# A graph layer on one core: all instruction orders replaced, and a restart charge in the planner

## The chip, the core and the metric

The kernel runs on one core of a Trainium2 chip. A core has five engines that run side by side, each with its own queue of instructions: TensorE (PE in the profile; its loading of the stationary matrix is listed apart as PEld), VectorE (DVE), ScalarE (ACT), GpSimd (POOL) and SyncE (SP), which here issues all the DMAs. An engine takes its instructions strictly in the order in which the program lists them, and waits on semaphores for what other engines produce. The metric is the device time in microseconds of one execution; less is better.

## The reference

For each of 64 graphs with 256 tokens of 768 features, the layer normalizes the tokens, multiplies them by three weight matrices, and sums over the edges of the graph in both directions:

```python
h = jnp.maximum(_layernorm(x, axis=-1), 0.0)
adj = heads.astype(hs.dtype); radj = jnp.swapaxes(adj, 1, 2)
ctx = jnp.matmul(adj, hs @ Wadj.T + badj) / deg_c[..., None]
ctx = ctx + jnp.matmul(radj, hs @ Wrev.T + brev) / rdeg_c[..., None]
ctx = ctx + hs @ Wself.T + bself
agg = jnp.einsum('bij,bijr->bir', adj, E[rels])
rel = agg @ Wr.T + br * deg[..., None]
...
return ctx + rel        # and x + that is the output
```

Adjacency and relation are the same 0/1 array, so that the relation terms come down to degrees of the tokens times a few fixed rows. (The kernel counts whether any other value occurs, and would then take a general path, which doesn't run here.)

## The kernel before, in words

**The mathematics.** A graph's tokens form two chunks of 128, `a` and `b`; the features form three blocks of 256 (`a0`, `a1`, `a2` and `b0`, `b1`, `b2`). The weights form three by three blocks. Instead of 18 block products for one image (that is, one graph) the kernel makes 15 (`PRODUCTS`, L24): GpSimd adds blocks of activations (L585), VectorE and ScalarE prepared sums of weight blocks once. For precision each operand is split into words (`split`, L590: ScalarE makes `left0`, VectorE `left1` and `left2`), and a product is three passes of four matmuls of 128x384: `first` and `second`, of 4 and 8 matmuls or the reverse, with a rescaling of the PSUM bank by ScalarE between them (`scale`, L657).

**The PSUM banks.** There are four double banks (class Q in `SLOTS`, L80). Several products share one, one after the other, and make a chain: x, y, z, w, t, u, v. After each product a `read` adds the bank into a result `c`: VectorE at L677 or L679, ScalarE at L668 for the first. The bank is free when the chain's last read is done.

**The two sweeps.** The weights of 15 products don't fit beside the rest, so there are two sweeps over the images. The first (`step1`) makes products 10, 5, 2, 8, 11, 14, 3 and 13 and stores five partial results and h in DRAM. Then the prepared weights are exchanged. The second (`step2`) loads them back, makes products 9, 7, 6, 15, 12, 4 and 1, adds the fixed rows (`rows`, L647), and multiplies by the adjacency: `aggregate` (L909) makes four groups of 8 matmuls (L917), `agg10`, `agg11`, `agg00` and `agg01`, from high and low words of `c` (ScalarE L901, GpSimd L905), each into a bank of its own that VectorE reads with L928. The first and the last image run in another way (`whole`, L754); the other 62 are regular.

**The front of an image** (`front1`): statistics (L698, L702), a power on GpSimd (L706), a transposition on PE (L709), a copy to DRAM and a broadcast back (`row`, L719), then GpSimd centres h (L728) and VectorE normalizes it (L732). In the second sweep there is a transposition of the degrees (L886).

**The order of the instructions** isn't written out. `record` (L416) lists every operation with its engine, an assumed duration, the buffers it reads and writes, and a due time, its `rank`: a time within the image plus the image's start. To each rank `Plan.op` (L270) adds an entry of the table `OFFSETS` (L91), by the kind of operation: `first 4` or `agg11` for all regular images alike, with suffixes `@`, `@1`, `$1` and `$` for the first two and last two images. Then `Plan.schedule` (L303) runs through modelled time: whenever an engine is idle, it takes from those operations whose inputs are known to be ready and whose buffers are free the one with the least rank; the engine is then idle again at the operation's modelled end less a fixed overlap (`OVERLAP`, L85; 0.17 us for PE). The order in which operations are picked is the order in which they are emitted, and so fixes the queue of every engine, SP's among them, and which buffer takes which slot.

Of the kernel before, what the change touches and what calls it, by code (L numbers as in the profile page):

```python
# [91 lines left out]
    "a0+a1+b0+b1": 8.69, "a0+a1+b0+b1$1": -108.02, "a0+a1+b0+b1@1": -28.72, "a0+a2": 3.05, "a0+a2$1": 18.41,  # L92
    "a0+a2+b0+b2": -1.59, "a0+a2+b0+b2$1": -102.81, "a0+a2+b0+b2@1": -29.55, "a0+a2+b2": -16.06,
    "a0+a2+b2$1": -82.94, "a0+a2+b2@1": 11.49, "a0+a2@1": -97.83, "a1+a2": -2.38, "a1+a2$1": -81.56,
    "a1+a2@1": -53.12, "a1+b0+b1": 2.88, "a1+b0+b1$1": -81.79, "a1+b0+b1@1": -139.93, "a1+b1": 4.34,
    "a1+b1$1": -79.5, "a1+b1@1": -17.92, "a2+b2": -15.53, "a2+b2$1": 11.35, "a2+b2@1": -111.63, "adj": 10.35,
    "adj$": -18.98, "adj$1": 7.21, "adj@": -54.66, "adj@1": 0.9, "agg00": 21.54, "agg00$": -40.97, "agg00$1": 40.2,
    "agg00@": -20.22, "agg00@1": -77.59, "agg01": 12.58, "agg01$": -138.03, "agg01$1": -97.46, "agg01@": -128.81,
    "agg01@1": -13.92, "agg10": 14.41, "agg10$": -22.12, "agg10$1": 69.43, "agg10@": -6.37, "agg10@1": 14.14,
    "agg11": 15.02, "agg11$": 11.68, "agg11$1": 35.7, "agg11@": -41.86, "agg11@1": -9.17, "aggr": 3.18,  # L100
    "aggr$": 7.69, "aggr$1": -25.58, "aggr@": -100.4, "aggr@1": -52.75, "b0+b1": 3.69, "b0+b1$1": 5.96,
    "b0+b1@1": -45.99, "b1+b2": -1.41, "b1+b2$1": -76.7, "b1+b2@1": -148.88, "b2-a1": -12.05, "b2-a1$1": -9.74,
    "b2-a1@1": -11.89, "bias": -84.06, "c00": 3.83, "c00$1": -110.03, "c00@": -5.48, "c00@1": -3.61, "c01": 5.97,
    "c01$1": 20.35, "c01@": 6.13, "c01@1": 11.64, "c02": 12.75, "c02$1": 7.61, "c02@": -3.44, "c02@1": -9.92,
    "c10": 17.9, "c10$1": 92.49, "c10@": 12.31, "c10@1": -26.9, "c11": 16.65, "c11$1": 30.73, "c11@": -0.83,
    "c11@1": -8.71, "c12": -9.52, "c12$1": 18.61, "c12@": 10.68, "c12@1": 6.4, "centre0": -2.78, "centre0$": 14.67,
    "centre0$1": 12.9, "centre0@": 1.93, "centre0@1": -4.77, "centre1": -29.85, "centre1$": 16.76,
    "centre1$1": 3.95, "centre1@": 34.71, "centre1@1": -3.19, "cols": -92.86, "d": 3.75, "d$": -46.21, "d$1": 7.75,
    "d@": 40.53, "d@1": -44.55, "degree": 14.27, "degree$": -21.1, "degree$1": -31.5, "degree@": -2.83,
    "degree@1": -21.54, "diagonal": 16.77, "eT": -7, "eps": -1.93, "eps$": -108.36, "eps$1": -19.3, "eps@": 4.64,  # L110
    "eps@1": 4.47, "first 1": 10.98, "first 1$1": 25.72, "first 10": 12.02, "first 10$1": -4.97,
    "first 10@1": 14.89, "first 11": 5.53, "first 11$1": -75.81, "first 11@1": 7.68, "first 12": -30.38,
    "first 12$1": -130.69, "first 12@1": -16.6, "first 13": 8.05, "first 13$1": -88.9, "first 13@1": -145.94,
    "first 14": -19.82, "first 14$1": 25, "first 14@1": 17.03, "first 15": -16.89, "first 15$1": -109.2,
    "first 15@1": -49.67, "first 1@1": 21.05, "first 2": 9.57, "first 2$1": -4.16, "first 2@1": 23.27,
    "first 3": -11.06, "first 3$1": -20.24, "first 3@1": -128.99, "first 4": 13.54, "first 4$1": 36.84,
    "first 4@1": -2.43, "first 5": 3.35, "first 5$1": -15.95, "first 5@1": -319.17, "first 6": 12.54,
    "first 6$1": -59.61, "first 6@1": -48.93, "first 7": -21.55, "first 7$1": -130.17, "first 7@1": -46.94,
    "first 8": -6.63, "first 8$1": -130.81, "first 8@1": 14.25, "first 9": -18.3, "first 9$1": -16.06,
    "first 9@1": -56.83, "flag": 69.83, "h0": -1.22, "h0$1": 11.51, "h0@1": -9.15, "h1": 0.44, "h1$1": 6.56,  # L120
    "h1@1": -11.86, "half0": 6.84, "half0$": -10.24, "half0$1": -105.95, "half0@": -17.91, "half0@1": -53.11,
    "half1": -7, "half1$": -161.34, "half1$1": -112.57, "half1@": -4.5, "half1@1": -33.45, "high00": -17.72,
    "high00$": 7.67, "high00$1": 39.71, "high00@": -95.79, "high00@1": -132.39, "high02": 15.43, "high02$": -8.98,
    "high02$1": -27.43, "high02@": -10.87, "high02@1": 13.62, "high10": -1.41, "high10$": -5.84,
    "high10$1": 105.73, "high10@": -88.55, "high10@1": 19.43, "high12": 7.31, "high12$": 13.34, "high12$1": -29.03,
    "high12@": -55.9, "high12@1": -47.34, "keep c00": 7.41, "keep c00$1": 27.77, "keep c00@": -65.27,
    "keep c00@1": -79.13, "keep c01": 1.55, "keep c01$1": -12.24, "keep c01@": 38.39, "keep c01@1": -91.42,
    "keep c02": -17.39, "keep c02$1": 38.98, "keep c02@": 62.12, "keep c02@1": -58.71, "keep c10": -12.45,
    "keep c10$1": -185.49, "keep c10@": -48.48, "keep c10@1": -47.03, "keep c11@": -2.5, "keep c12": -22.45,
    "keep c12$1": 31.13, "keep c12@": -22.62, "keep c12@1": -25.9, "keep h0": -33.37, "keep h0$1": -2.51,  # L130
    "keep h0@1": -48.37, "keep h1": 16.04, "keep h1$1": -14.04, "keep h1@1": -19.88, "left0 1": 5.55,
    "left0 1$1": 15.94, "left0 10": 5.84, "left0 10$1": 4.52, "left0 10@1": -47.34, "left0 11": -32.11,
    "left0 11$1": -11.52, "left0 11@1": -104.63, "left0 12": 3.78, "left0 12$1": 33.37, "left0 12@1": -32.14,
    "left0 13": 3.38, "left0 13$1": 16.36, "left0 13@1": 9.79, "left0 14": 7.42, "left0 14$1": -64.24,
    "left0 14@1": 10.25, "left0 15": 6.36, "left0 15$1": 11.31, "left0 15@1": 10.98, "left0 1@1": -28.48,
    "left0 2": 9.1, "left0 2$1": -6.48, "left0 2@1": 9, "left0 3": -20.81, "left0 3$1": -158.45,
    "left0 3@1": -7.38, "left0 4": -7.17, "left0 4$1": 35.5, "left0 4@1": -1.66, "left0 5": -38.77,
    "left0 5$1": -42.67, "left0 5@1": -48.2, "left0 6": 2.23, "left0 6$1": 18.1, "left0 6@1": -2.29,
    "left0 7": -20.33, "left0 7$1": -43.73, "left0 7@1": -83.4, "left0 8": 2.58, "left0 8$1": -65.87,
    "left0 8@1": -23.62, "left0 9": -38.94, "left0 9$1": -103.7, "left0 9@1": -23.48, "left1 1": 13.87,  # L140
    "left1 1$1": -156.93, "left1 10": -33.63, "left1 10$1": -20.33, "left1 10@1": -75.44, "left1 11": 1.26,
    "left1 11$1": -21.37, "left1 11@1": -66.88, "left1 12": 0.51, "left1 12$1": 27.39, "left1 12@1": -125.37,
    "left1 13": 10.94, "left1 13$1": -237.77, "left1 13@1": 13.62, "left1 14": -7.94, "left1 14$1": -95.64,
    "left1 14@1": 17.17, "left1 15": -0.1, "left1 15$1": -0.79, "left1 15@1": -32.31, "left1 1@1": -26.63,
    "left1 2": -36.76, "left1 2$1": 8.05, "left1 2@1": -94.05, "left1 3": 2.6, "left1 3$1": 24.12,
    "left1 3@1": -171.62, "left1 4": 2.22, "left1 4$1": 6.46, "left1 4@1": -19.24, "left1 5": -20.28,
    "left1 5$1": -16.74, "left1 5@1": 10.07, "left1 6": -1.47, "left1 6$1": 16.61, "left1 6@1": -34.54,
    "left1 7": -12.59, "left1 7$1": 14.19, "left1 7@1": 7.51, "left1 8": 9.77, "left1 8$1": 15.63,
    "left1 8@1": 3.29, "left1 9": 3.68, "left1 9$1": -113.48, "left1 9@1": -52.25, "left2 1": -30.23,
    "left2 1$1": -170.63, "left2 10": -8.63, "left2 10$1": -27.62, "left2 10@1": 10.3, "left2 11": 5.94,  # L150
    "left2 11$1": 20.71, "left2 11@1": -162.72, "left2 12": -13.41, "left2 12$1": -131.98, "left2 12@1": -3.75,
    "left2 13": 8.66, "left2 13$1": 7.67, "left2 13@1": -6.15, "left2 14": -16.62, "left2 14$1": 10.35,
    "left2 14@1": 0.48, "left2 15": 8.03, "left2 15$1": 33.15, "left2 15@1": -19.54, "left2 1@1": -38.48,
    "left2 2": -3.09, "left2 2$1": 9.07, "left2 2@1": -23.95, "left2 3": 3.29, "left2 3$1": -104.5,
    "left2 3@1": -23.03, "left2 4": 8.23, "left2 4$1": -58.03, "left2 4@1": -16.99, "left2 5": -19.18,
    "left2 5$1": -2.15, "left2 5@1": -31.63, "left2 6": -22.08, "left2 6$1": -105.49, "left2 6@1": -1.79,
    "left2 7": 6.73, "left2 7$1": -71.09, "left2 7@1": 10.22, "left2 8": 6.26, "left2 8$1": 14.18,
# [1096 lines left out]
```

## Time and profile before

| what | us |
|---|---|
| median of 3 runs | 2518.97 (2517.87 to 2520.16) |
| the profiled execution, its own time | 2519.23 |
| span of that execution, first to last instruction | 2517.3 |

The span is divided into 40 slices; each digit is the busy share of an engine in tenths:

```profile
PE   7999999999999999999999999999999999999998
DVE  7887778777777877778899999999999999999997
ACT  4788888888888888886666666666666666666664
POOL 1555555555555555542555555555555555555553
PEclk9999999999999999999999999999999999999999
```

The first sweep fills slices 2 to 18, then come two or three slices of exchange, then the second sweep. The largest groups of matmuls, with the count, the busy time and the mean duration of one:

```profile
L623 PE MATMUL y<-word,left 128*128 128x384 f32 x2976 | 573.2, 337 | 0.0
L917 PE MATMUL agg<-hl,a 128*128 128x384 f32 x2048 | 398.8, 338 | 0.1
L928 DVE SCALAR_TENSOR_TENSOR c<-agg,rd,c 128x768 f32<-128x768 f32 x252 | 252.8, 1003 | 28.7 <-PE agg L917 28.5
```

The matmuls overlap each other in the record: a duration of 337 ns doesn't mean that they follow each other at that distance. The last column is the engine's idle time just before the group and what ended it.

### The profile page before, as it was taken

The page shows a single profiled execution, that of the slowest core. Times are in us where ns is not written, and L with a number is a line of the kernel's source. Part 1 is how long each engine was busy: PE and PEld are TensorE (multiplying, and loading weights), DVE is VectorE, ACT ScalarE, POOL GpSimd, SP SyncE. Part 2 cuts the span into 40 slices and gives each one's busy share as a digit, 9 for nine tenths or more (in the row PEclk, how much of TensorE's full clock was granted, in tenths as well). Part 3 has the DMA queues.
Part 4 walks back from the last instruction along what each step waited for, and adds up shares of the span by engine and source line. Part 5 has one row for each costly group of instructions (what it writes and reads, how often), then busy time and mean ns, then how long its engine had stood idle before and what let it go on. Part 6 is the DMA issues. An engine that isn't in the chain of part 4 may idle for free. (4 is left out here: it accounts for less than half of the span.)

```text
span 2517.3 us, 43767 instructions
## 1 busy us (share of the span) xinstructions
PE 2489.2 (99%) x13922; PEld 2412.2 (96%) x13922; DVE 2134.8 (85%) x3933; ACT 1814.3 (72%) x3901; POOL 1300.7 (52%) x1138
## 2 busy tenths in 40 slices
PE   7999999999999999999999999999999999999998
PEld 4899999999999999997999999999999999999998
DVE  7887778777777877778899999999999999999997
ACT  4788888888888888886666666666666666666664
POOL 1555555555555555542555555555555555555553
PEclk9999999999999999999999999999999999999999
DMA  5677777777777777785676666667666666766663
GB/s 209 244 275 282 265 267 285 272 264 274 279 268 269 283 274 270 278 295 189 190 226 213 210 210 207 209 212 213 212 209 206 213 210 211 212 211 211 216 212 130
DMA packets 223971, 590.64 MB, mean 235 GB/s; under 512 B 24036, under 2 KB 24292, under 8 KB 223736
## 3 DMA queue, kind: packets, MB, share of 16 engines
q1 hardware_dynamic: 223736, 587.79, 69.0%
q8 instruction: 112, 1.84, 0.3%
q14 instruction: 123, 1.01, 0.1%
HBM read 364.22 MB, written 223.48 MB: 233 GB/s over the span
## 5 line engine op out<-in xcount | busy, mean ns | idle before, releaser
L905 POOL TENSOR_TENSOR hl<-c,hl 128x768 fp32r<-128x768 f32 x256 | 490.5, 1936 | 400.1 <-ACT hl L901 347.5
L623 PE MATMUL y<-word,left 128*128 128x384 f32 x2976 | 573.2, 337 | 0.0
L623 PE MATMUL x<-word,left 128*128 128x384 f32 x2976 | 570.8, 336 | 1.5 <-ACT x L657 1.0
L623 PEld LDWEIGHTS y<-word,left 128*128 128x128 f32 x2976 | 521.3, 188 | 5.5 <-ACT y L657 0.4
L623 PEld LDWEIGHTS x<-word,left 128*128 128x128 f32 x2976 | 521.1, 188 | 4.5 <-ACT x L657 1.6
L917 PE MATMUL agg<-hl,a 128*128 128x384 f32 x2048 | 398.8, 338 | 0.1
L917 PEld LDWEIGHTS agg<-hl,a 128*128 128x128 f32 x2048 | 356.0, 188 | 15.0 <-DVE c L679 14.5
L728 POOL TENSOR_TENSOR h<-h,row 128x768 f32<-128x768 f32 x128 | 235.6, 1861 | 246.7 <-DMA row<-d 207.1
L901 ACT ACTIVATE hl<-c 128x768 fp32r<-128x768 f32 x256 | 203.2, 839 | 154.9 <-PE agg L917 142.6
L623 PE MATMUL w<-word,left 128*128 128x384 f32 x1488 | 304.1, 339 | 1.3 <-DVE x L776 1.3
L623 PE MATMUL z<-word,left 128*128 128x384 f32 x1488 | 301.2, 337 | 0.3 <-ACT left L595 0.2
L928 DVE SCALAR_TENSOR_TENSOR c<-agg,rd,c 128x768 f32<-128x768 f32 x252 | 252.8, 1003 | 28.7 <-PE agg L917 28.5
L657 ACT ACTIVATE x<-x 128x768 f32<-128x768 f32 x248 | 197.4, 796 | 96.6 <-PE x L623 95.0
L612 DVE SCALAR_TENSOR_TENSOR left<-left 128x256 fp32r<-128x256 f32 x434 | 266.0, 634 | 0.0
L623 PEld LDWEIGHTS z<-word,left 128*128 128x128 f32 x1488 | 260.2, 188 | 3.7 <-ACT left L595 0.5
L623 PEld LDWEIGHTS w<-word,left 128*128 128x128 f32 x1488 | 258.3, 188 | 4.4 <-DVE x L776 1.6
L657 ACT ACTIVATE y<-y 128x768 f32<-128x768 f32 x248 | 197.2, 795 | 43.4 <-PE y L623 40.2
L612 DVE SCALAR_TENSOR_TENSOR left<-left,top 128x256 fp32r<-128x256 f32 x496 | 199.8, 413 | 6.4
L677 DVE TENSOR_TENSOR c<-c,v 128x768 f32<-128x768 f32 x124 | 117.3, 946 | 81.2 <-PE v L647 79.5
L585 POOL TENSOR_TENSOR a1+a<-h 128x256 f32<-128x256 f32 x62 | 45.9, 740 | 271.1 <-DMA h<-kept_h 249.7
L602 ACT ACTIVATE top<-left 128x256 f32<-128x256 f32 x496 | 181.3, 383 | 6.0 <-DVE left L612 2.0
L706 POOL TENSOR_TENSOR cols<-cols,half 128x2 f32<-128x2 f32 x64 | 82.7, 1292 | 166.4 <-DVE cols L705 164.7
(137 smaller groups left out, 4441.4 us busy)
## 6 DMA issues: line engine op xcount, KB each, us to landing
c<-kept SPq DMA_DIRECT2D x316, 384.0 KB
kept<-c SPq DMA_DIRECT2D x252, 384.0 KB
x<-in_x_dram SPq DMA_DIRECT2D x128, 384.0 KB
h<-in_x_t_dram SPq DMA_DIRECT2D x128, 384.0 KB
out_dram<-c SPq DMA_DIRECT2D x126, 384.0 KB
kept_h<-h SPq DMA_DIRECT2D x124, 384.0 KB
h<-kept_h SPq DMA_DIRECT2D x124, 384.0 KB
adj<-in_adj_dram SPq DMA_DIRECT2D x64, 512.0 KB
```

Of the source, the lines that this page charges most:

```text
L585: lambda: nc.gpsimd.tensor_tensor(t(home), x[1](), y[1](), op=op),
L602: lambda: nc.scalar.activation(view(top), t(w)[:, 0].bitcast(F32), AF.Copy),
L612: lambda: nc.vector.scalar_tensor_tensor(t(w)[:, 2], t(w)[:, 1].bitcast(F32), -STEP, first(), op0=ALU.mult, op1=ALU.add), s == 1,
L623: nc.tensor.matmul(t(q)[:, half, : H // 2], t(w)[:, lw, f, :], t(r[rw])[:, f, ts(half, H // 2)], start=start and i == 0 and f == 0, stop=s ...
L657: lambda: nc.scalar.activation(view(), view(), AF.Copy, scale=scale),
L677: emit = lambda to=to, op=op: nc.vector.tensor_tensor(to(), to(), view(), op=op)
L706: pool(0.7, r - 21.5, f"pow {b}", [col], [col], lambda: nc.gpsimd.tensor_tensor(var(), var(), v["half"], op=ALU.pow))
L728: lambda h=h, one=one: nc.gpsimd.tensor_tensor(t(h), t(h), one(0), op=ALU.subtract),
L901: lambda: nc.scalar.activation(t(pair)[:, 0], t(o), AF.Copy, scale=LOWER),
L905: lambda: nc.gpsimd.tensor_tensor(t(pair)[:, 1], t(o), t(pair)[:, 0].bitcast(F32), op=ALU.subtract),
L917: nc.tensor.matmul(t(q)[:, half, : H // 2], t(s["a"])[:, c, k, ts(ic, P)], t(pairs[c])[:, part, ts(half, H // 2)], start=(c == 0 and part ...
L928: lambda q=q, to=to, ic=ic: nc.vector.scalar_tensor_tensor(to(), t(q)[:, :, : H // 2], t(rd)[:, ic, k : k + 1], to(), op0=ALU.mult, op1=AL ...
```

## The change

Two things are changed. In `Plan.schedule`, an operation of PE that is picked later than PE's modelled end of idleness is taken to last 0.1 us longer. And every number of `OFFSETS`, 777 entries under the same names, is replaced. No operation, duration, buffer or due time besides is touched. The lines of the diff for the entries that the text speaks of, and the edit of the planner:

```diff
 OFFSETS = {
...
-    "agg00@": -20.22, "agg00@1": -77.59, "agg01": 12.58, "agg01$": -138.03, "agg01$1": -97.46, "agg01@": -128.81,
-    "agg01@1": -13.92, "agg10": 14.41, "agg10$": -22.12, "agg10$1": 69.43, "agg10@": -6.37, "agg10@1": 14.14,
-    "agg11": 15.02, "agg11$": 11.68, "agg11$1": 35.7, "agg11@": -41.86, "agg11@1": -9.17, "aggr": 3.18,
...
+    "agg00@1": -2.07, "agg01": 17.2, "agg01$": -13.99, "agg01$1": -22.76, "agg01@": -70.15, "agg01@1": -11.71,
+    "agg10": 13.48, "agg10$": 14.67, "agg10$1": -41.77, "agg10@": 3.9, "agg10@1": -43.3, "agg11": 14.32,
...
+    "wr": 6.55, "x0": -3.18, "x0$": -12.39, "x0$1": -15.93, "x0@": -81.58, "x0@1": -15.47,
 }
...
                     if b.slot is None:
                         b.slot = free[b.cls].pop(0)
                         order[b.cls].remove(b)
-                o.start, o.end = now, now + o.took
+                late = 0.1 if e == "PE" and now > idle[e] + 1e-5 else 0.0
+                o.start, o.end = now, now + o.took + late
                 if e == "SP":
                     queue = max(queue, now) + o.took
                     o.end = queue + o.lands
```

Some regular entries, before and after:

| entry | before | after |
|---|---|---|
| `agg10` | 14.41 | 13.48 |
| `agg11` | 15.02 | 14.32 |
| `agg00` | 21.54 | 10.32 |
| `agg01` | 12.58 | 17.20 |
| `read 1` | -8.92 | 18.59 |
| `read 9` | -11.49 | 7.98 |
| `first 12` | -30.38 | 17.40 |
| `turn2` | -13.17 | -0.62 |

## The prediction

> **What bounds the kernel now.** I read the page's busy line first, then the busy time by stage, then the waits of TensorE's weight loader, and last the order of time around the one wait that recurs.
>
> ```profile
> PE 2489.2 (99%) x13922; PEld 2412.2 (96%) x13922; DVE 2134.8 (85%) x3933; ACT 1814.3 (72%) x3901; POOL 1300.7 (52%) x1138
> ```
>
> TensorE (PE) leaves 28.1 us of the 2517.3 us span. That is an upper bound of what any order can win only if "busy" meant full speed, so I look at how many matmuls each stage gets through.
>
> ```profile
> core 0: us, PE busy (x) PEld busy (x) DVE busy (x) ACT busy (x) POOL busy (x), PEclk, DMA share, GB/s
> 100.00:1100.00 1000.00, 999.90 (x5740) 991.47 (x5739) 790.01 (x1718) 841.09 (x1718) 547.46 (x531) 1.00 0.74 274
> 1220.00:2440.00 1220.00, 1219.93 (x6949) 1201.74 (x6948) 1103.87 (x1839) 798.96 (x1837) 645.60 (x516) 1.00 0.68 211
> ```
>
> The two rows are the first sweep and the second sweep over the 62 regular images. PE is busy without a gap in both, yet its weight loader (PEld) is busy 99.1% of the first and 98.5% of the second. The clock is at full speed. The second row also shows VectorE (DVE) at 1103.9 of 1220 us, 90%.
>
> ```profile
> PEld agg L917 <- DVE c L679: 14.0, 56, 0.4
> ```
>
> This is the only line of the loader's waits between 1220 and 2440 us: once per image the weight loads of an aggregation wait for VectorE's read of a PSUM bank. In time order, PE, its loader and VectorE around one such place:
>
> ```profile
> 1505.35 1.55 PE L623 MATMUL x<-word,left 128*128 128x384 f32 x8
> 1506.74 3.17 PE L917 MATMUL agg<-hl,a 128*128 128x384 f32 x16
> 1509.75 0.27 PE L886 MATMUL pt<-ident,cols 128*128 128x128 f32 x1
> 1509.77 0.94 PE L623 MATMUL v<-word,left 128*128 128x384 f32 x4
> ...
> 1506.57 1.40 PEld L917 LDWEIGHTS agg<-hl,a 128*128 128x128 f32 x8
> 1508.23 1.35 PEld L917 LDWEIGHTS agg<-hl,a 128*128 128x128 f32 x8 [0.26 <-DVE c L679]
> ...
> 1506.37 0.94 DVE L677 TENSOR_TENSOR c<-c,x 128x768 f32<-128x768 f32 x1
> 1507.23 0.94 DVE L679 SCALAR_TENSOR_TENSOR c<-x,c 128x768 f32<-128x768 f32 x1
> 1508.10 0.15 DVE L883 TENSOR_SCALAR rd<-deg 128x4 f32<-128x4 f32 x1
> ```
>
> Eight matmuls take 1506.74 - 1505.35 = 1.39 us, 0.1735 each, and their last end is seen at 1.55. Sixteen without a stop would show 1.55 + 1.39 = 2.94 us; the aggregation pair shows 3.17. So **one stall costs 0.23 us** although PE never looks idle. The cause is a queue on VectorE: the last product of chain x ends at 1506.90, but its read (L679) starts only when another read (L677, started 0.86 us earlier) lets VectorE go; the read ends at 1508.17 and the loader restarts at 1508.23.
>
> **Floors.** A transpose delays its successors by 0.02 + (0.94 - 0.85) = 0.11 us (the four x matmuls that follow at 1510.55 show 0.85). An image has 96 wide matmuls in the first sweep and 84 + 32 + 4 = 120 in the second, each with one transpose. First stage: 5681 x 0.1735 + 59 x 0.11 = 992 of 1000 us. Second: 6892 x 0.1735 + 57 x 0.11 = 1202 of 1220. So 8 and 18 us lie above the floor, and 56 x 0.23 = 12.9 of the 18 are this stall.
>
> **The edges.**
>
> ```profile
> PE whole L765 <- DVE h L732: 10.3, 1, 10.3
> PE pt L709 <- POOL cols L706: 7.8, 1, 7.8
> PE w L623 <- DVE x L776: 1.3, 1, 1.3
> ```
>
> These lead PE's own waits. The first two are the start: PE's matrix work begins at 18.52 us, behind the load, statistics, row broadcast and normalization of the first image, a chain of dependencies that no order shortens much. Between 1100 and 1220 us, where the weights are exchanged, the loader's waits add up to 3.4 us in eight lines; after 2440 us to 4.3 us. No line of PE's or its loader's waits names a DMA. After the last matmuls come one read of 1.02 us (L928, ending at 2512.45) and 4.85 us of store and closing.
>
> [...]
>
> **The change part by part.** (1) The planner's charge for a PE operation that starts after PE's modelled idle time rises by 0.1 us. It emits nothing: 13922 matmuls, all VectorE, ScalarE and GpSimd instructions and all DMAs stay. It is worth 0 by itself, except that later modelled ends move, so ready times and picks do too. (2) All 777 offsets change, so every queue, SP's single DMA queue included, is put in another order. The sum by place:
>
> - The recurring stall: between -12.9 (gone) and 0 (kept). It can go by order alone: had VectorE read chain x before the other read, from 1506.90 to 1507.84, the loader would have been ready by its own 1506.57 + 1.39 = 1507.96. The new charge bears on exactly such places: a modelled bubble once per image is multiplied by 62, and now counts 0.1 more each. I take -12.9. Against it: the offset of the read in question (`read 1`) goes from -8.92 to 18.59, later, while `agg11` stays (15.02 to 14.32), so the cure would have to come from another bank, not from an earlier read.
> - Stalls that the new order brings in the regular images: none to 12.9 for one per second-sweep image in full. With 2.0 us of VectorE slack in 21.2 us (10% of the image) some are likely, since reads of 0.87 us each stand ahead of PE operations of 0.69 or 1.39 us. I take a quarter of one, 0.06 us an image, 3.2 us.
> - First sweep: VectorE is at 79%, ScalarE at 84%, and the loader's named waits are 0.6 us in 1000. At best half of its 8 us goes, at worst one stall per image comes, 14. I take 0.
> - Edges: at best the 3.4 + 4.3 + 1.3 us shrink by half, -4.5; at worst a load or a weight word late at the start or the exchange adds as much as 8. I take 0.
> - DMA order: SP waits often, the longest total being 269.0 us for buffers before L856's loads, but no PE wait follows from it now. 0 while loads keep their lead; an image late by 1 us costs 1 us, once, or 62 if each is late.
>
> Sum: -12.9 + 3.2 = -9.7. Against the profiled execution's own 2519.23 that is 2509.5; the median of the runs, 2518.97, lies 0.3 below that execution, which I leave out.
>
> **The rivals.**
>
> - A, the forecast: the recurring stall goes and little takes its place. 2503 (all of it, and 3 at the edges) to 2514; likeliest 2509.5. For it: one cause, one place, one read in the way. Chance 0.50.
> - B, nothing to tell: the charge alters the planner's accounts, but the order found has about as many real stalls, the aggregation's or another's. 2519, give or take 5. For it: the stall is 0.23 us and the planner must get a read's start right within 0.3 us. Against it: a search over all orders is unlikely to land on the very same price. Chance 0.26. Part of it falls on either side.
> - C, slower: VectorE in the second sweep becomes what PE waits for, twice or more per image. The reads bunch (the lines above have two in a row, each 0.87 us from start to start) and two banks come free late where one did; the old stall goes or stays, net at least one more: 62 x 0.23 = 14.3, so 2533.5, up to 2548 with two more. It decides from two stalls per image on. For it: 90% busy, and a wholly new order. Against it: 10% of slack is two reads' worth, and the order before got by with one stall. Chance 0.24; its light form, a fraction of an image's stall or a worse exchange, begins at 2524.
>
> **How the numbers follow.** 0.2% is 5.0 us, about what a measurement of this kernel can tell from no change. Faster (under 2514): 0.47 from A and 0.05 from B = 0.52. Same: 0.03 from A, 0.20 from B, 0.02 from C = 0.25. Slower (over 2524): 0.01 from B and 0.22 from C = 0.23. The range runs from 2503, with 0.04 below it, to 2527, above which most of C lies, about 0.15. A's own range is 2503 to 2514.
>
> **What would show it.** Right: the loader's waits between 1220 and 2440 us no longer have a line with 56 waits on VectorE, its busy time nears 99.2% of that stage, and the second sweep's period falls from 21.23 us (1508.23 to 1529.46, two restarts of the loader) to about 21.0. Wrong as in B: a line of 50 to 120 waits under another name and the same period. Wrong as in C: two or more such lines, a period above 21.4. The first sweep should still pass 574 to 577 matmuls per 100 us, PE's first matrix work should start at 18 to 20 us, and the exchange should hold under 8 us of loader waits; a later start or longer exchange would make the prediction wrong at the edges instead.

## The result: 45.7 us slower, and the profile after

| what | before | after |
|---|---|---|
| median of 6 runs each, us | 2518.48 (2517.63 to 2520.16) | 2564.15 (2563.33 to 2565.69) |
| span of the profiled execution, us | 2517.3 | 2562.0 |
| image period in the second sweep, us | 21.25 | 21.91 |

The ratio is 1.0181, with a 95% interval of 1.0168 to 1.0194. The image period is the mean distance from one transposition of the degrees to the next between 1220 and 2440 us. The same number of instructions runs on every engine. The busy line of the page after:

```profile
PE 2519.2 (98%) x13922; PEld 2425.2 (95%) x13922; DVE 2202.1 (86%) x3933; ACT 1816.9 (71%) x3901; POOL 1245.4 (49%) x1138
```

VectorE is 67 us busier with the same 3933 instructions: some of them last longer. GpSimd is 55 us less busy. The two sweeps of after, in the same view of busy time by stage as before:

```profile
core 0: us, PE busy (x) PEld busy (x) DVE busy (x) ACT busy (x) POOL busy (x), PEclk, DMA share, GB/s
100.00:1100.00 1000.00, 1000.00 (x5709) 996.61 (x5709) 885.53 (x1700) 843.60 (x1707) 508.08 (x530) 1.00 0.79 272
1220.00:2440.00 1220.00, 1205.08 (x6735) 1166.67 (x6734) 1045.93 (x1777) 770.45 (x1781) 610.66 (x502) 1.00 0.59 205
```

There are two losses. In the second sweep 6735 matmuls start where 6949 did, and the loader has fallen from 1201.7 to 1166.7 us: PE waits. In the first sweep 5709 start where 5740 did, although PE is busy throughout and the loader shows *more* time, 996.6 against 991.5: each matmul has become a little slower. By the starts of the matmuls, the first product of the second sweep begins at 1189.4 us instead of 1183.4 (+6.0), and the last matmul of all starts 1366.1 us after it instead of 1327.7 (+38.5); from there to the end it is 6.4 us instead of 6.3. That is the 44.7 us of the span. The clock column stays at 1.00 in both sweeps.

The loader's waits in the second sweep of after, between 1220 and 2440 us (every line number after the planner's edit is one higher than before):

```profile
PEld pt L887 <- DVE c L680: 31.1, 56, 1.1
PEld v L648 <- ACT half L893: 19.6, 56, 0.4
PEld x L624 <- DVE c L678: 0.4, 1, 0.4
PEld agg L918 <- DVE c L929: 0.2, 1, 0.2
```

The aggregation's line, `PEld agg L917 <- DVE c L679: 14.0, 56, 0.4` before, is gone, as forecast. Two lines have come: the transposition of the degrees waits for a read by VectorE, and the fixed rows wait for what ScalarE makes of the transposition. The timeline of one such place in after:

```profile
1701.64 1.02 DVE L929 SCALAR_TENSOR_TENSOR c<-agg,rd,c 128x768 f32<-128x768 f32 x1
...
1701.87 1.85 POOL L906 TENSOR_TENSOR hl<-c,hl 128x768 fp32r<-128x768 f32 x1 [4.75 <-ACT hl L902]
...
1702.58 1.18 DVE L883 COPY cols<-deg 128x8 f32<-128x8 f32 x1
...
1702.85 1.57 PE L624 MATMUL u<-word,left 128*128 128x384 f32 x8
...
1703.66 0.95 DVE L680 SCALAR_TENSOR_TENSOR c<-x,c 128x768 f32<-128x768 f32 x1
...
1704.64 0.85 ACT L902 ACTIVATE hl<-c 128x768 fp32r<-128x768 f32 x1 [0.79 <-DVE c L680]
1704.66 0.14 PEld L887 LDWEIGHTS pt<-ident,cols 128*128 128x128 f32 x1 [0.56 <-DVE c L680]
...
1704.75 1.64 PE L624 MATMUL x<-word,left 128*128 128x384 f32 x8
...
1705.39 0.79 ACT L658 ACTIVATE u<-u 128x768 f32<-128x768 f32 x1
...
1706.12 0.55 ACT L893 ACTIVATE half<-pt 64x128 fp32r<-64x128 f32 x2
...
1706.43 0.30 PEld L648 LDWEIGHTS v<-rows,half 128*128 128x128 f32 x2 [0.36 <-ACT half L893]
```

The line to look at is the copy. It moves 8 numbers per partition and takes 1.18 us. It starts while GpSimd subtracts (from 1701.87 to 1703.72) and ends 0.04 us after that. Behind it in VectorE's queue stands the read of a bank (L680), which therefore ends at 1704.61 and not about a microsecond earlier; the transposition, ready at 1704.66 - 0.56 = 1704.10, needs that bank. ScalarE's next operation waits for the same read (0.79 us, L902), so that the two halves behind it are late too, and the rows with them. One long copy, two waits. The same copy in the two kernels, by the view of one source line (duration in ns, least, median and greatest; first and last start), before and after:

```profile
L882 DVE COPY cols<-deg x64: 156/161/170, 1134.0 to 2478.2; 128x8 f32<-128x8 f32 x64
```

```profile
L883 DVE COPY cols<-deg x64: 147/1165/1831, 1158.2 to 2523.0; 128x8 f32<-128x8 f32 x64
```

So the copy takes 161 ns before, where 63 of the 64 stand clear of GpSimd, and 1165 ns in after. Sorted by their starts and ends in the trace of after, 59 of the 64 copies start during a subtraction and last over a microsecond, and each of these ends 27 to 35 ns after that subtraction does. Such an instruction is called held below, which says that it lasted longer beside GpSimd and no more: what stops it, no trace here shows. The kernel before had its own instance, cheaper: the third words of the operands (`left<-left`, L612, 128x256) take 0.41 us free and 2.05 us in the 59 cases that start during GpSimd's subtraction, ending 0.28 us after it.

So, by place, for one second-sweep image in time between matmul starts: transposition +0.46, rows +0.31, the aggregation's stall -0.20, and +0.09 for the remaining matmuls, which follow each other a little more slowly. Together that is the 0.66 us by which the period grew.

### The profile page after: what moved, and what is told of

The parts are those of the page before. It is cut to its first block, busy times and chain, and to the rows that moved or that the text cites. A ratio compares the mean times of both kernels' runs of the same rounds, so it can differ in the third digit from the quotient of the medians.

```text
span 2562.0 us, 43480 instructions
## 1 busy us (share of the span) xinstructions
PE 2519.2 (98%) x13922; PEld 2425.2 (95%) x13922; DVE 2202.1 (86%) x3933; ACT 1816.9 (71%) x3901; POOL 1245.4 (49%) x1138
## 5 line engine op out<-in xcount | busy, mean ns | idle before, releaser
L906 POOL TENSOR_TENSOR hl<-c,hl 128x768 fp32r<-128x768 f32 x256 | 475.2, 1868 | 712.5 <-ACT hl L902 707.2
L624 PE MATMUL y<-word,left 128*128 128x384 f32 x2976 | 591.5, 340 | 0.0
L624 PE MATMUL x<-word,left 128*128 128x384 f32 x2976 | 587.2, 338 | 0.5 <-DVE c L680 0.4
L918 PE MATMUL agg<-hl,a 128*128 128x384 f32 x2048 | 389.6, 337 | 0.0
L733 DVE SCALAR_TENSOR_TENSOR h<-h,row 128x768 f32<-128x768 f32 x128 | 216.3, 1690 | 36.7 <-POOL h L729 36.7
L902 ACT ACTIVATE hl<-c 128x768 fp32r<-128x768 f32 x256 | 208.4, 837 | 50.7 <-DVE c L680 49.7
L707 POOL TENSOR_TENSOR cols<-cols,half 128x2 f32<-128x2 f32 x64 | 46.0, 719 | 365.7 <-DVE cols L706 303.5
L613 DVE SCALAR_TENSOR_TENSOR left<-left,top 128x256 fp32r<-128x256 f32 x496 | 205.9, 416 | 6.3
L678 DVE TENSOR_TENSOR c<-c,x 128x768 f32<-128x768 f32 x124 | 117.8, 950 | 70.6 <-PE x L624 68.5
```

The source lines that it names most:

```text
L613: lambda: nc.vector.scalar_tensor_tensor(t(w)[:, 2], t(w)[:, 1].bitcast(F32), -STEP, first(), op0=ALU.mult, op1=ALU.add), s == 1,
L624: nc.tensor.matmul(t(q)[:, half, : H // 2], t(w)[:, lw, f, :], t(r[rw])[:, f, ts(half, H // 2)], start=start and i == 0 and f == 0, stop=s ...
L678: emit = lambda to=to, op=op: nc.vector.tensor_tensor(to(), to(), view(), op=op)
L707: pool(0.7, r - 21.5, f"pow {b}", [col], [col], lambda: nc.gpsimd.tensor_tensor(var(), var(), v["half"], op=ALU.pow))
L733: lambda h=h, one=one: nc.vector.scalar_tensor_tensor(t(h), t(h), 0.0, one(1), op0=ALU.max, op1=ALU.mult), True,
L902: lambda: nc.scalar.activation(t(pair)[:, 0], t(o), AF.Copy, scale=LOWER),
```

## The experiments

Two theories stood against each other for the second sweep. In one, the copy held by GpSimd's subtraction makes the loss. In its rival, the new order itself is too tight (reads in the way, as my slower rival had it), and the copy only fills time in which VectorE would have waited anyway. For the first sweep's loss there was a third: the order also decides which slot a tile gets, and so its address.

**Which half of the change.** The planner's edit alone, on the old table; and the new table without the edit.

```diff
-                o.start, o.end = now, now + o.took
+                late = 0.1 if e == "PE" and now > idle[e] + 1e-5 else 0.0
+                o.start, o.end = now, now + o.took + late
```

> The table of offsets as before, only the planner's charge of 0.1 us added. It leaves the regular images' order as it was: TensorE's order differs from before in 495 of 13763 matmuls, all around the exchange of the weights. Theory (the new table brings the loss): 2518 us, give or take 3, with the 56 waits of the aggregation on VectorE unchanged. Rival (the charge itself spoils the order): at least 2540 us.

Measured: 2656.49 us, ratio 1.0546 (1.0530 to 1.0562). The theory, 2518 us, was wrong and its rival right: on the old table the charge costs 138 us. My expectation was wrong about the order too: besides the exchange, each second-sweep image has its transposition four matmuls earlier, one pair of VectorE reads swapped and a store swapped with a load. Timeline of one place in it:

```profile
1716.77 3.91 POOL L906 TENSOR_TENSOR hl<-c,hl 128x768 fp32r<-128x768 f32 x2 [1.52 <-ACT hl L902]
1716.91 2.08 DVE L609 TENSOR_TENSOR left<-h,left 128x256 fp32r<-128x256 f32 x1
...
1718.91 2.05 DVE L613 SCALAR_TENSOR_TENSOR left<-left 128x256 fp32r<-128x256 f32 x1
...
1721.88 1.68 PE L624 MATMUL t<-word,left 128*128 128x384 f32 x8 [1.56 <-DVE c L678]
```

Two subtractions follow each other on GpSimd, and two 0.41 us instructions of VectorE are held, one by each, and last 4.1 us in all; before, only one of a pair was. PE waits 1.56 us for the read queued behind.

> The new table of offsets without the planner's charge. Its order differs from the changed kernel's in three VectorE instructions near the exchange of the weights. Theory (the charge acts through the search for the table alone; the table is what runs): 2560 to 2568 us. Rival: more than 5 us from the changed kernel's 2564.

Measured: 2564.74 us, 1.0186 (1.0169 to 1.0203), the same as with the edit. In the kernel after it is the table that counts. If the charge had a part in how that table was found, no run here shows it.

**The swapped pair put back** into the kernel of the first experiment, in 59 images:

```diff
-        for o in plan.schedule():
+        order = plan.schedule()
+        for o in [o for o in order if o.eng == "DVE" and o.name.startswith("read 7 ")]:
+            at = order.index(o)
+            back = [p for p in order[:at] if p.eng == "DVE"][-1]
...
+                order.remove(back)
+                order.insert(order.index(o) + 1, back)
+        for o in order:
```

> The kernel of the charge alone (2656 us), with one pair of VectorE instructions put back in the order of the kernel before in 59 images: the read of chain v (L678) ahead of the last aggregation's read (L929). The transposition of the degrees stays four matmuls earlier and SP's store and load stay swapped. In the trace of the charge alone, VectorE stands idle 2.4 us for that aggregation, comes 1.3 us later to its left operands, and two of them then last 2.08 and 2.05 us beside GpSimd's two subtractions. Theory (that pair alone moves VectorE into GpSimd's window): 2516 to 2526 us. Rival (the earlier transposition or SP's swap): above 2600 us.

Measured: 2676.79 us, 1.0627 (1.0610 to 1.0643). A miss: the pair is not what brings VectorE beside the subtractions. The earlier transposition and the swapped store and load are left; which of them starts it was not tried.

**The copy put elsewhere.** The kernel after, with the copy of each image issued just behind its twin, the comparison of the same degrees (L882); 119 VectorE places differ, nothing else.

```diff
-        for o in plan.schedule():
+        order = plan.schedule()
+        for o in [o for o in order if o.name.startswith("tok")]:
+            first = next(p for p in order if p.name == o.name)
+            if o is not first:
+                order.remove(o)
+                order.insert(order.index(first) + 1, o)
+        for o in order:
```

> The changed kernel, but VectorE's small copy into the columns (0.16 us alone, 1.16 us in the changed kernel) is issued one place earlier, right after its twin, and so ahead of GpSimd's 1.85 us subtraction instead of beside it. Nothing else is moved. Theory (the copy stands still behind GpSimd for 1.0 us, VectorE's read of chain x is late by that, and with it the PSUM bank of the transposition and the fixed rows): the copy is back at 0.16 us, the transposition's waits (32.8 us at the loader) go, the rows' waits (20.7 us) go in large part, and the time is 2521 to 2530 us. Rival (the new table puts transposition and rows too close behind what they need, whatever the copy does): the rows' waits stay near 20 us and the time is above 2543 us.

Measured: 2525.76 us, 1.0031 (1.0019 to 1.0043), 38.4 less than after. Its loader's waits between 1220 and 2440 us:

```profile
PEld x L624 <- DVE c L678: 3.2, 7, 0.5
PEld x L624 <- ACT x L658: 1.5, 9, 0.2
PEld pt L887 <- DVE c L680: 1.1, 1, 1.1
PEld v L648 <- ACT half L893: 0.3, 1, 0.3
```

Both lines of 56 waits have shrunk to single ones, the period is 21.26 us, against 21.25 in the kernel before, and the held copy accounts for 38.4 us, 0.65 us for each of 59 images. The first sweep is as slow as in after.

**The copy in another form, in its old place.** A maximum over an axis of length one gives the same numbers.

```diff
-        dve(0.2, r - 2.0, f"tok {b}", degs, [(col, 1)], lambda: nc.vector.tensor_copy(to(3), of()))
+        dve(0.2, r - 2.0, f"tok {b}", degs, [(col, 1)], lambda: nc.vector.tensor_reduce(to(3), of().unsqueeze(4), AX.X, ALU.max))
```

> The changed kernel with the same order; VectorE's copy of the degrees is made by a reduction over an axis of length one instead, the same 8 numbers at the same place. [...] Theory (the wait belongs to this instruction's form, not to its place): the reduction takes 0.2 us or less beside GpSimd and the time is 2520 to 2532 us, as with the copy one place earlier. Rival (any VectorE instruction there waits, or the place in the order is what costs): 2558 us or more.

Measured: 2524.70 us, 1.0025 (1.0016 to 1.0033). The order is untouched here, so the rival, an order too tight in itself, has no room left. The source line of it:

```profile
L883 DVE TENSOR_REDUCE cols<-deg x64: 136/157/162, 1159.3 to 2483.7; 128x8 f32<-128x8 f32 x64
```

In this form the 8 numbers take 157 ns, and 162 at most, nearly always beside a subtraction, where the copy took 1165. The next small instruction of VectorE's queue, the tensor_scalar for `rd` some 4.6 us later, now starts in 59 images while GpSimd adds blocks, and lasts 740 ns instead of 158 (in the kernel after 261 instead of 163); no line of the loader's waits comes of it.

**The addresses.** In the compiled programs I looked up each product matmul's two operand addresses and set them against the distance to the next matmul's start in the trace, leaving out the distances that hold a wait or a transposition:

```
share, mean distance both alike (mod 64)                one at 0, other at 32
before               77%: 174.1 ns (both at 0)          22%: 176.3 to 176.5 ns
after                66%: 175.3 ns (both at 32)         34%: 176.4 ns
```

A slot is as large as the largest tile that the order puts into it. In the old order an early one of the small slots only ever gets tiles of 96 bytes, which happens to bring nearly all later tiles back to multiples of 64. In the new order that slot also gets tiles of 512 bytes, and the small slot with tiles of 96 bytes alone comes late: all left operands and two thirds of the words stay at 32, the other words are at 0. To test it, the tiles are moved and nothing else: a pad of 32 bytes, and the small slots opened at full size, in the kernel after and in the kernel before. The same edit without the pad puts all operands of before 32 bytes off.

```diff
+        pool.tile([P, 8], F32, name="pad")
+        for i in range(SLOTS["S"]):
+            pool.tile([P, P], F32, tag=f"S{i}", name=f"whole_S{i}")
         for col in fixed["cols"]:
```

> The changed kernel with the same order on every engine; only the places of its buffers in on-chip memory are moved by 32 bytes or so, by one pad and by giving the six small slots their full size at once. In the changed kernel all left operands and two thirds of the words begin 32 bytes off a multiple of 64; here all begin at a multiple of 64. In the traces of both kernels, matmuls with both operands at such multiples follow each other at 174.0 ns, those with one off at 176.4 to 176.7, those with both off at 175.3 on average. Theory (the address makes the matmuls slower): the first sweep loses about 1.9 ns on each of 5952 matmuls, 11 us, the second up to 10 us more, so 2543 to 2554 us, and the first sweep passes 575 matmuls per 100 us again. Rival (the slower pace is an after-effect of VectorE's and GpSimd's timing, not of the addresses): 2561 to 2567 us.

Measured: 2545.96 us, 1.0108 (1.0093 to 1.0124): 18.2 less than after, with both waits still there (32.8 and 19.5 us).

> The kernel before with the same order and the same move of its buffers to multiples of 64 bytes. There 77% of the matmuls had both operands at such multiples already. Theory (addresses): the mean distance falls from 174.6 to 174.0 ns over 13464 matmuls, 7 to 8 us, so 2510 to 2513 us. Rival (no effect of the addresses): 2518 us, give or take 2.

Measured: 2513.38 us, 0.9980 (0.9971 to 0.9988): 5.1 less than before, with the aggregation's wait still there (15.0 us).

> The kernel before, same order, with all words, left operands and adjacency tiles moved so that every one begins 32 bytes off a multiple of 64. Theory (each operand that begins off a multiple of 64 costs): the mean distance rises to some 175.3 ns or more, against 173.9 with all at multiples, so 2524 to 2535 us. Rival (what costs is that the two operands of a matmul disagree): 2510 to 2516 us, as with all at multiples. Third (addresses don't matter, the run with all at multiples was faster for another reason): 2518 us.

Measured: 2514.59 us, 0.9984 (0.9976 to 0.9992). With both operands 32 bytes off the kernel is within 1.2 us of the one with both at multiples of 64 (2514.59 against 2513.38); before, where 22% disagree, took 2518.48. So it was the disagreement, not the 32 bytes, that went with the loss here. The busy time by stage, first sweep, of the kernel after aligned, and of before shifted:

```profile
100.00:1100.00 1000.00, 1000.00 (x5784) 994.30 (x5783) 890.02 (x1720) 853.11 (x1726) 516.70 (x537) 1.00 0.83 275
```

```profile
100.00:1100.00 1000.00, 999.73 (x5761) 990.24 (x5760) 794.45 (x1723) 843.06 (x1722) 549.23 (x534) 1.00 0.74 274
```

5709 and 5740 matmuls in these 1000 us have become 5784 and 5761. In the three kernels whose operands all agree the products' matmuls follow each other at 173.7 to 174.0 ns.

**Both cures together**, the copy early and all operands, the degrees' columns too, at multiples of 64:

> The changed kernel with the copy one place earlier (2525.8 us) and all operands, the degree columns included, at multiples of 64 bytes. Theory (the two causes are apart and add up): 2525.8 - 18 to 20 = 2504 to 2510 us. Rival (with the copy's wait gone, VectorE or ScalarE keeps the second sweep at its pace, and only the first sweep gains its 11 us): 2512 to 2516 us.

Measured: 2508.96 us, 0.9959 (0.9944 to 0.9974), faster than both kernels. Its second sweep in the view by stage:

```profile
1220.00:2440.00 1220.00, 1219.75 (x6978) 1205.94 (x6977) 1058.03 (x1848) 788.44 (x1845) 650.48 (x519) 1.00 0.62 211
```

Against the second sweep of the aligned kernel before (6951 matmuls), by the distances of matmul starts: the aggregation's stall is gone, -12.4 us (116 longer distances, two per image); a distance of 0.25 instead of 0.174 us after an aggregation has come 56 times, +4.1; somewhat slower matmuls, +2.8, which I didn't follow up.

**The forecast's cure by order.** The prediction said that VectorE could read chain x before the other read and the aggregation's stall would go. In the kernel before, the two reads are exchanged in 59 images (the edit is that of the swapped pair above, with `read 1 ` and `read 9 `).

> The kernel before, with VectorE's read of product 1 (L679, it frees the bank of chain x for the aggregation) issued ahead of the next image's read of product 9 (L677) in 59 images; nothing else moved. Theory of the prediction (0.23 us per image lie in that pair of reads): the aggregation's 56 waits go, 59 x 0.23 = 13.6 us, so 2503 to 2509 us. Rival (the read put back is late by 0.9 us for the next product of its own chain, or VectorE meets GpSimd at another place): 2516 us or more.

Measured: 2647.19 us, 1.0508 (1.0493 to 1.0522). The aggregation's line is gone, and in its place between 1220 and 2440 us:

```profile
PEld u L623 <- DVE c L928: 93.6, 52, 1.8
PEld pt L886 <- DVE c L928: 36.5, 52, 0.7
```

The timeline shows the same as that of the first experiment:

```profile
1701.72 2.40 DVE L612 SCALAR_TENSOR_TENSOR left<-left 128x256 fp32r<-128x256 f32 x2
1701.79 4.02 POOL L905 TENSOR_TENSOR hl<-c,hl 128x768 fp32r<-128x768 f32 x2 [4.13 <-ACT hl L901]
...
1705.11 1.35 PEld L623 LDWEIGHTS u<-word,left 128*128 128x128 f32 x8 [1.84 <-DVE c L928]
```

`left<-left` is held 117 times now, 59 before. To see how much of this is GpSimd's doing, its subtraction was replaced by a memset, in this kernel and in the kernel before. The low words of the aggregation's operand are left out there; the matmuls on them still run.

```diff
-            lambda: nc.gpsimd.tensor_tensor(t(pair)[:, 1], t(o), t(pair)[:, 0].bitcast(F32), op=ALU.subtract),
+            lambda: nc.gpsimd.memset(t(pair)[:, 1].bitcast(F32), 0.0),
```

> The kernel with the two reads exchanged (2647 us), GpSimd's subtraction of 1.85 us that makes the low words for the aggregation replaced by setting them to zero: the low words are left out of the result, the order of every engine is the same. In its trace one left operand per image, 0.41 us alone, lasts 2.04 us beside GpSimd where the kernel before had that once and here has it twice, and the awaited reads follow it. Theory (the exchange itself is good, and the collision with GpSimd made it slow): the left operands are back at 0.41 us, the aggregation doesn't wait, and the time is 2498 to 2515 us. Rival (the exchange of the reads delays the next product's chain): above 2600 us.

> The kernel before with the same replacement, as the measure for the run above: the low words of the aggregation are left out. Theory: the one collision per image goes, VectorE gains 1.6 us per image, the aggregation's wait of 0.23 us may stay or go: 2503 to 2519 us. Rival (shorter GpSimd work makes no difference to a kernel bound by TensorE): 2519 us with the 56 waits unchanged. Either way, if this run and the one above are within 15 us of each other, the exchange of the reads is not what cost 128 us.

Measured: 2549.19 us, 1.0124 (1.0107 to 1.0141), and 2511.27 us, 0.9970 (0.9960 to 0.9981). The first missed what either theory gave. With the subtraction the exchange costs 2647.19 - 2518.48 = 128.7 us, without it 2549.19 - 2511.27 = 37.9, so that some 91 us of it go with the subtraction. The 37.9 us stand under these names (exchanged reads without the subtraction, 1220 to 2440 us):

```profile
PEld pt L886 <- DVE c L928: 39.3, 56, 0.7
PEld u L623 <- DVE c L928: 9.9, 56, 0.2
```

So the exchange moves the wait to the transposition's bank even where `left<-left` is not held (0.43 us at most here). In before without the subtraction, the aggregation's wait is gone (0.6 us in two). That old stall very likely had the same origin: the timeline of before shows a held instruction 10 us ahead of the stall at 1508.23, with VectorE busy without a stop from there to the late read.

```profile
1497.05 4.05 POOL L905 TENSOR_TENSOR hl<-c,hl 128x768 fp32r<-128x768 f32 x2 [1.54 <-ACT hl L901]
1497.30 2.07 DVE L612 SCALAR_TENSOR_TENSOR left<-left 128x256 fp32r<-128x256 f32 x1
```

A memset takes 0.74 us and a subtraction 1.86, so these two kernels differ in GpSimd's load besides the held instructions, and what the shorter load alone does was not tried.

## Why the prediction was wrong

The change of 45.7 us is a chain of four measured pairs: aligning before -5.1; from there to the new order, aligned and with the copy out of the way, 2508.96 - 2513.38 = -4.4; taking the alignment away 2525.76 - 2508.96 = +16.8; putting the copy back +38.4.

- **"The recurring stall ... I take -12.9"**: right in that the line is gone. By the distances between matmul starts the stall had cost 0.20 us an image, not 0.23, which is 11.6 us in the kernel before and 12.4 in the aligned one.
- **"Stalls that the new order brings in the regular images ... I take a quarter of one, 0.06 us an image, 3.2 us"**: this is the step that failed. With the copy moved to where it is short, the new order's own stalls came to 4.1 us, near the term. But the term stood on VectorE's durations in the trace of before. A copy of 0.16 us was taken to stay one wherever it is put; beside GpSimd's subtraction it lasted 1.17, and 38.4 us came of it, twelve times the term. The table of before showed the hint: one line's durations from 386 to 2079 ns. I read means and missed it.
- **"It is worth 0 by itself, except that later modelled ends move"**, of the planner's charge: on the new table so, where the time without it is 0.6 us off. On the old one picks do move, and it costs 138 us.
- **"First sweep ... I take 0"**: wrong by 6.0 us in the start of the second sweep, and the second sweep has its share too: 16.8 us from addresses, a cost that was in no case. That no buffer is touched is true of the list of buffers; which slot each one gets, and so its place, did change.
- **Edges** and **DMA order**, 0 each: right. No wait of PE names a DMA, and from the last matmul's end to the end of the span it is 6.1 us, against 5.9.
- **"It can go by order alone"**, by an earlier read of chain x: shown wrong in that form; the wait moved to another bank and the held instructions doubled.
- **The rivals**: C named what happened, VectorE's late reads in two places per image, a period longer by more than 0.46 us. But it had reads that bunch as the cause and 2533.5 to 2548 as its reach. Reads from PSUM lasted as long beside GpSimd as without it, before and after (0.95 and 0.94 us); it was an operation on eight columns that was held (1.17 us instead of 0.16).

## What to carry to other kernels

Before trusting that an order costs what a planner with fixed durations says, look in the trace for instructions whose greatest duration is several times the median, and see what the other engines do at those moments: on VectorE here these were, beside GpSimd's subtraction, the degrees' copy (in after 1179 ns in the mean instead of 163) and `left<-left` (in before 2053 instead of 412), beside its centring of h the normalization (in after 2558 instead of 949), and beside its addition of blocks the tensor_scalar for `rd` (740 instead of 158 in the kernel with the reduction). Two things helped the copy: put ahead of the subtraction, it took the kernel from 2564.15 us to 2525.76, and as a reduction, which was not held, to 2524.70.

This planner does have a term for such meetings: all of GpSimd's operations, and in the regular images VectorE's normalization (L733) and the left words of the second sweep (L609, L613), carry the mark `lock`, and none of them is picked while another one runs in modelled time (L337). The degrees' copy and tensor_scalars carry no such mark, so beside a subtraction the copy looked free to it. What marking it would give was not tried, and the mark works in modelled time alone: `left<-left` carries it and was held 59 times in the kernel before.

And where an order decides the slots, check the addresses too: the first sweep of after passed 5709 matmuls in 1000 us with PE busy throughout and the clock at 1.00, and 5784 once its operands lay alike again.

## What the runs showed that I had not expected

- **In these kernels the pace of a product's matmuls went with whether their two operands start alike modulo 64 bytes**: 173.7 to 174.1 ns where they do (both at 0, or both 32 bytes off) and 176.3 to 176.5 where not, 1.4%. It is read off the addresses in the compiled programs and the starts in the traces, and off the runs with moved tiles (18.2 us less than after, 5.1 and 3.9 less than before); why it is so, nothing here shows. Three things stay open. In after the agreeing pairs, which stand among disagreeing ones, ran at 175.3. In the aggregations of after, by the slots that the planner gives out, 735 disagreeing pairs (stationary at 0, moving at 32) ran at 175.0. And a matmul's moving operand may as well have to agree with the stationary matrix of the next one: sorted so, the products of before show the same, 174.1 against 176.3 to 176.6.
- **Not every VectorE instruction was held.** Sorted by whether GpSimd worked at their start, reads from PSUM (0.94 and 0.95 us), the statistics (0.55 and 0.55), the few reciprocals there were (164 to 179 ns) and the reduction kept their durations; in after the copies went from 163 to 1179 ns in the mean, and with the reduction in place the tensor_scalars from 158 to 740.
- **Being held was not by itself a loss.** In the first sweep of after, 59 of the 128 normalizations start while GpSimd centres h and are held for 1.6 us each (2.56 us instead of 0.95), which the source view shows only in its greatest duration, and PE waits for none of them:

```profile
L733 DVE SCALAR_TENSOR_TENSOR h<-h,row x128: 921/952/2595, 17.4 to 1128.7; 128x768 f32<-128x768 f32 x128
```
